# Linear attention and a gated FFN in one kernel: another order at the start and between the two parts, woven tiles in mid-sequence, and finish_b by pairs of groups

## The chip, the cores and the metric

The kernel runs on one core of one Trainium2 chip. The metric is the time of one execution in microseconds (us) on the device, less being better. Three runs of the kernel before gave a median of 2803.57 us (2799.61 to 2805.04). One further execution was profiled; it took 2802.45 us, of which the profiled span, from the first instruction to the last, is 2800.6 us.

The core has five engines with a queue each, which they work through in order: TensorE (PE in the profile: matmuls and transposes; its weight loads, PEld, overlap them), VectorE (DVE), ScalarE (ACT), GpSimd (POOL) and SyncE (SP), which here only issues DMAs. The other engines can issue DMAs too, from their own queues.

## The reference

The input x is 16 sequences of 1024 rows of 512 numbers. A linear attention with 16 heads of 32 comes first, then a gated FFN; after each, x is added and a layernorm is taken.

```python
qkv = x @ Wqkv.T + bqkv
q, k = rmsnorm(q, gq), rmsnorm(k, gk)             # over all 512
q, k = apply_rope(q), apply_rope(k)               # pairs (even, odd) by cos, sin
qf, kf = relu(q), relu(k)                         # 16 heads of 32
vk = einsum('bhlp,bhld->bhpd', [v, 1], kf)        # per sequence and head: 33 x 32
res = einsum('bhpd,bhld->bhlp', vk, qf)
attn = res[..., :-1] / (res[..., -1:] + 1e-6)
x = layernorm(x + rmsnorm(attn @ Wout.T + bout, gout))
# FFN; x_prev is x one row up, zero at a sequence's first row
xk = mu_k * x + (1 - mu_k) * x_prev
xr = mu_r * x + (1 - mu_r) * x_prev
out = layernorm(x + sigmoid(xr @ W_r.T) * (relu(xk @ W_k.T)**2 @ W_v.T))
```

## The kernel before

**Tiles and products.** The rows lie in N = 128 tiles of 128 rows; a sequence is 8 tiles, a group of the FFN NT = 4 tiles. Weights and activations are each split into a high and a low part in fp32r, and every product is three matmuls (high by high, high by low, low by high), usually 128x512, so 12 for a tile and a 512x512 weight. A cast on ACT makes the high part, a subtraction on DVE or POOL the low one. A scheduler puts the instructions of each engine in an order by its own simulated times; the program's order is its starting point. Eight semaphores serve the DMAs.

**Part one, `slot(i)` for each tile i (L563).** `proj` (L370) makes q and k of the tile: the bias has been copied into the PSUM bank by ACT before (`seeded`, L132, called the seed here), so the twelve matmuls add to it. `rope` (L417) squares q and k on ACT for the norm, multiplies them on DVE by two tables each (L425 into a tile called t2, L426 into ro), adds, and stores q to DRAM. The tables are the norm's weight times cos and sin. `tables(i)` (L394) computes them on POOL for the first eight tiles (L409, L412) and stores them in DRAM (tab_d, L413); from tile 8 on they are loaded (L404). `add_kx` (L449, matmuls pskx at L462) adds k^T x of tile i - 1 to a sum over the sequence, from the split k (kh on ACT, L438, kl on DVE, L439) and the split x (xnh, xnl). The four PSUM banks of that sum leave four banks, taken in turn, for everything else in part one.

**The end of a sequence.** v is never made per tile: `finish_a` (L472) copies the sum kx out of PSUM and splits it, `finish_s` (L480) makes the sum of k, `finish_b` (L494) multiplies by v's weights (pskv, L505 and L513), adds v's bias times the sum of k, applies the mask of heads and splits, in four column groups; `finish_c` (L531, psm at L538) multiplies one group each by the output weight and stores the result m in DRAM (m_d). In slots: finish_a and finish_s stand in the slot two after the sequence's last tile (9 + 8b for sequence b), finish_b in the next, finish_c in the four from 11 + 8b on.

**Woven tiles.** The attention's second step for a tile reads q and m back: `part_q` (L186, ends with L197 on DVE) divides by the denominator, `part_qt` (L201) transposes q (psqt, L138) and splits it (qth on ACT, L208, qtl on DVE, L209), `part_s` seeds the bank with the output bias, `part_m` multiplies by m (psy, L153), and `part_y` (L242) norms (the square on ACT is named junky, L247), adds x and takes the layernorm in place. For the first NPRE = 7 tiles this is begun inside part one: tile j's loads in slot FIRST + STEP j (40, 48, ...), part_q one slot later; for j < 4 the whole step follows there.

**The bridge.** After the last slot: w_k is loaded from DRAM, tiles 4 to 6 are completed, `turn` (L627) transposes x of group 0 (pst, L138) and `mix_t` (L633, ACT L637, DVE L638, split L648 and L649) makes the mixed x for k; the last sequence's ends stand between these and part_fk of group 0. Then w_r is loaded, group 0 is turned a second time for r, and tiles 7 and 8 are begun ahead with sequence 0's and 1's m.

**Part two.** For each group s, part_fk (psk), part_fr (psr) and part_fv (psv), all at L153, are woven with the attention's second step of the tiles two groups ahead (part_y's steps at L235 to L252) and with `part_t` (turn and both mixes) of the next group.

**The start.** In before, ACT's queue issues the loads of b_qk, of half of the weights, then of g_qk, cos, sin, b_out, g_out, mu and bv; the weights of q and then of k are split in four row blocks each (high part on ACT, low on POOL); then come tables(0) and seed(0).

Of the kernel before, what the change touches and what calls it, by code (L numbers as in the profile page):

```python
# [21 lines left out]
NPRE = 7  # L22
FIRST, STEP = 40, 8
XA = 7
XB = 4
# [8 lines left out]
def kernel(  # L34
# [221 lines left out]
    with ExitStack() as a_ctx:  # L256
# [49 lines left out]


# [5 lines left out]
        split_x(0)  # L313
        b_qk = ca.tile([P, 2 * DIM], F32, name="b_qk")
        nc.scalar.dma_start(out=b_qk, in_=bqkv[0 : 2 * DIM].partition_broadcast(P))
        for j in range(2):
            cols = slice(j * DIM, (j + 1) * DIM)
            for c in range(NC_):
                n = NC_ * j + c
                split_w(  # L320
                    w_qk["h"][:, c, cols],
                    w_qk["l"][:, c, cols],
                    wqkv[:, c, cols],
                    (V, G)[c % 2],
                    (nc.sync, nc.scalar)[c % 2],
                    *(("x", XA), ("q", 3))[n >= XA],
                )
        load_xt(1)
        load_xn(0)
        g_qk = wp.tile([P, 2 * DIM], F32, tag="m", bufs=NC_, name="g_qk")  # L330
        nc.scalar.dma_start(out=g_qk, in_=gqk.partition_broadcast(P))
        cos = ca.tile([P, 8, HH], F32, name="cos")
        nc.scalar.dma_start(out=cos, in_=cos_t)
        sin = ca.tile([P, 8, HH], F32, name="sin")
        nc.scalar.dma_start(out=sin, in_=sin_t)

        sn = ca.tile([P, 8, 2, HH], F32, name="sn")
        G.tensor_copy(sn[:, :, 0, :], sin)
        G.tensor_scalar(sn[:, :, 1, :], sin, -1.0, None, ALU.mult)
        nc.scalar.dma_start(out=b_out, in_=bout.partition_broadcast(P))  # L340
        nc.scalar.dma_start(out=g_out, in_=gout.partition_broadcast(P))
        mu, omm = {}, {}
        for n, m in (("k", mu_k), ("r", mu_r)):
            mu[n] = const.tile([P, NC_], F32, name=f"mu_{n}")
            nc.scalar.dma_start(out=mu[n], in_=m)
            omm[n] = const.tile([P, NC_], F32, name=f"omm_{n}")
            V.tensor_scalar(omm[n], mu[n], -1.0, 1.0, ALU.mult, ALU.add)

        bv = te.tile([P, NC_], F32, name="bv")
        with nc.allow_non_contiguous_dma(reason="512 numbers"):  # L350
            nc.scalar.dma_start(
                out=bv, in_=bqkv[2 * DIM : 3 * DIM].rearrange("(g p) -> p g", p=P)
            )
# [26 lines left out]
        first = {}  # L380

        def seed(i):
            for j in range(2):
                first[i, j] = seeded(f"ps{'qk'[j]}{i}", b_qk[:, j * DIM : (j + 1) * DIM])

        def rows(tl):
            return tl.rearrange("p (h i) -> p h i", i=HH)

        def halves(tl):
            return tl.rearrange("p (h two i) -> p h two i", two=2, i=HH)  # L390

        tab, tab_d = {}, {}

        def tables(i):  # L394

            t = i % 8
            if i < 8:
                tab_d[t] = dram.tile([P, 2, 2, DIM], F32, name=f"tab_d{t}")
            for j in range(2):
                for n in range(2):  # L400
                    tb = wa.tile([P, DIM], F32, tag=f"tab{j}{n}", name=f"tab{j}{n}{i}")
                    tab[i, j, n] = tb
                    if i >= 8:
                        nc.sync.dma_start(out=tb, in_=tab_d[t][:, j, n, :])  # L404
                        continue
                    g = g_qk[:, j * DIM : (j + 1) * DIM]
                    if n == 0:
                        c = cos[:, t, :].unsqueeze(1).to_broadcast([P, 2 * HEADS, HH])
                        G.tensor_mul(rows(tb), rows(g), c)  # L409
                    else:  # L410
                        c = sn[:, t, :, :].unsqueeze(1).to_broadcast([P, HEADS, 2, HH])
                        G.tensor_mul(halves(tb), halves(g), c)  # L412
                    nc.sync.dma_start(out=tab_d[t][:, j, n, :], in_=tb)  # L413

        acc, ros = {}, {}

        def rope(i, ps):  # L417
# [3 lines left out]
            for j in range(2):  # L421
                S.activation(junk(f"{i}{j}"), ps[j], AF.Square, accum_out=ss[:, j : j + 1])
                r = wa.tile([P, DIM], F32, tag=f"ro{j}", bufs=1 + j, name=f"ro{j}{i}")
                t2 = wa.tile([P, DIM], F32, tag="t2", name=f"t2{j}{i}")
                V.tensor_mul(t2, ps[j], tab.pop((i, j, 1)))  # L425
                V.tensor_mul(r, ps[j], tab.pop((i, j, 0)))  # L426
                V.tensor_add(halves(r), halves(r), halves(t2)[:, :, ::-1, :])
                ro.append(r)
                if j == 0:
                    q_d[i] = dram.tile([P, DIM], F32, name=f"q_d{i}")  # L430
                    nc.sync.dma_start(out=q_d[i], in_=r)
# [62 lines left out]
        def finish_b(b):  # L494
# [4 lines left out]
            for g in range(NC_):  # L499
# [4 lines left out]
                for c in range(NC_):  # L504
# [16 lines left out]
                kv = te.tile([P, P], F32, tag="kv", bufs=1, name=f"kv{b}{g}")  # L521
                V.scalar_tensor_tensor(
                    kv, ks[:, cols], bv[:, g : g + 1], ps[:, 0:P], ALU.mult, ALU.add
                )
                V.tensor_add(kv, kv, ps[:, P : 2 * P])
                V.tensor_mul(kv, kv, mask)
                S.copy(th[:, g, :], kv)
                V.tensor_sub(tl[:, g, :], kv, f32(th[:, g, :]))
# [30 lines left out]

        tables(0)  # L560
        seed(0)

        def slot(i):  # L563
            if i + 2 < N:
                load = load_xt(i + 2)
            b, t = divmod(i - 2, 8)
            if i - 2 >= 0 and t == 7:
                finish_a(b)
            if i < N:
                qk = [proj(i, 0), proj(i, 1)]  # L570
            if i + 1 < N:
                split_x(i + 1)
            if i < N:
                split_xn(i)
            if i + 1 < N:
                load_xn(i + 1)
            if i - 2 >= 0 and t == 7:
                finish_s(b)
            if i - 3 >= 0 and (i - 3) % 8 == 7:
                finish_b((i - 3) // 8)  # L580
            if i - 11 >= 0 and (i - 11) % 8 < NC_ and i < N:
                finish_c((i - 11) // 8, (i - 11) % 8)
            if 0 <= i - 1 < N:
                add_kx(i - 1)
            if i < N:
                state[i] = rope(i, qk)
            if i + 1 < N:
                tables(i + 1)
                seed(i + 1)
            if 1 <= i and late and i < N:  # L590
                late_weight()
            j, late_by = divmod(i - FIRST, STEP)
            if 0 <= j < NPRE:
                if late_by == 0:
                    with tc.issue_after(load.ins):
                        if j == 0:
                            load_ks(0)
                            for c in range(NC_):
                                load_m(0, c)
                        load_q(j)  # L600
                        load_x(j)
                    if j < NT:
                        part_s(j)
                if late_by == 1:
                    part_q(j)
                    if j < NT:
                        part_qt(j)
                        part_y(j, part_m(j))
# [55 lines left out]
        def part_fk(s, o):  # L664
# [10 lines left out]
            kh = wm.tile([P, HT], F32R, tag="kah", bufs=5, name=f"kah{s}{o}")  # L675
            kl = wm.tile([P, HT], F32R, tag="kal", bufs=5, name=f"kal{s}{o}")
# [4 lines left out]

        load_w("k", cb)
        for j in range(NT, NPRE):
            part_s(j)
        for c in range(NC_):
            turn(0, c)
            mix_t(0, c, "k")
        slot(N)
        for j in range(NT, NPRE):
            part_qt(j)  # L690
            part_y(j, part_m(j))
        slot(N + 1)
        part_fk(0, 0)
        part_fk(0, 1)
        slot(N + 2)
        part_fk(0, 2)
        part_fk(0, 3)
        tk_ctx.close()
        tx_ctx.close()
        wb = ctx.enter_context(tc.tile_pool(name="workb", reuse_waits="tile", bufs=1))  # L700
        wr = ctx.enter_context(tc.tile_pool(name="workr", reuse_waits="tile", bufs=1))
        own["ks"] = wr
        load_w("r", wr)
# [3 lines left out]
        )  # L707
        for g in range(NC_):
            finish_c(NB - 1, g)
        for c in range(NC_):  # L710
            turn(0, c)
            mix_t(0, c, "r")
        early = range(NPRE, 2 * NT + 1)
        load_ks(1)
        for j in early:
            load_q(j)
        load_q(2 * NT + 1)
        ps_m = {}
        for j in early:
            if j < 2 * NT:  # L720
                part_s(j)
            part_q(j)
            part_qt(j)
            if j < 2 * NT:
                ps_m[j] = part_m(j)

    wc = ctx.enter_context(tc.tile_pool(name="workc", reuse_waits="tile", bufs=1, side="right"))
    own["x"] = own["m"] = wc
    w_f["v"] = wc.tile([P, NC_, 2, DIM], F32R, name="w_v")

    def part_fr(s, t):
# [7 lines left out]
        gate[s, t] = wr.tile([P, DIM], F32, tag="gate", bufs=4, name=f"gate{s}{t}")  # L739
# [31 lines left out]
    for j in early:  # L771
        load_x(j)
    for c in range(NC_):
        load_m(1, c)
    for j in ps_m:
        part_y(j, ps_m[j])
    load_w("v", wc)
    for s in range(NH):
# [100 lines left out]
```

## Time and profile before

| | us |
|---|---|
| median of three runs | 2803.57 |
| profiled execution / its span | 2802.45 / 2800.6 |
| PE busy | 2728.1 (97%) |
| DVE / ACT / POOL busy | 2201.8 / 1893.1 / 735.8 |
| mean granted clock of PE | 0.994 |

A row of groups or of the timeline names the engine, the line, the operation and its output and inputs by the program's names. Of a wait, the engine, the tile and the instruction waited for are named. The granted clock is the share of full speed that the throttle gave PE in a window: 12 matmuls of 128x512 take 2.77 us at full clock and about twice that at half. The chain is the work that ended last, followed back from the end.

### The profile page before, as it was taken

How to read it: one execution, taken by the hardware profiler on the slowest of the kernel's cores; microseconds unless marked ns; L12 is line 12 of the kernel's file. 1: busy time of each engine (PE TensorE's matmuls, PEld its weight loads, DVE VectorE, ACT ScalarE, POOL GpSimd, SP SyncE). 2: the span in 40 equal slices, each digit the busy share in tenths (PEclk: the TensorE clock that was granted, in tenths of full speed). 3: DMA queues.
4: the chain of work that ended last, by engine and by line, in shares of the span. 5: the costliest groups of instructions: out<-in, count | busy, mean ns of one | idle time of the engine just before them, and what ended most of it. 6: DMA issues, size and time to landing. Idle time of an engine off the chain costs nothing.

```text
span 2800.6 us, 40329 instructions
## 1 busy us (share of the span) xinstructions
PE 2728.1 (97%) x12536; PEld 2236.0 (80%) x12536; DVE 2201.8 (79%) x4966; ACT 1893.1 (68%) x3839; POOL 735.8 (26%) x808
## 2 busy tenths in 40 slices
PE   7999999999999999988999999999999999999998
PEld 5788877777888888866788888888888888888887
DVE  7988877777888788866778787878787878788774
ACT  5566655555555566655777777777777777777775
POOL 6422221221222222222322222222222222222221
PEclk9999999999999999999999999999999999999999
DMA  7787776666777777755323222232323132313210
GB/s 245 234 294 254 236 256 204 213 209 202 231 237 238 237 230 237 231 176 176 104 70 106 95 77 92 92 110 65 106 91 113 57 113 84 110 65 106 76 57 30
DMA packets 230854, 431.17 MB, mean 154 GB/s; under 512 B 24544, under 2 KB 24800, under 8 KB 230640
## 3 DMA queue, kind: packets, MB, share of 16 engines
q1 hardware_dynamic: 228384, 425.85, 46.9%
q10 hardware_dynamic: 2256, 2.76, 0.3%
q8 instruction: 99, 1.62, 0.2%
q14 instruction: 115, 0.94, 0.1%
HBM read 313.14 MB, written 115.38 MB: 153 GB/s over the span
## 4 chain that ended last, share of the span: by engine, by line
PE 76%; DVE 1%; DMA 1%; ACT 1%; issue 0%; POOL 0%; SPq 0%; POOLq 0%; ACTq 0%; DVEq 0%
PE psk L153 13%; PE psv L153 12%; PE psy L153 12%; PE psr L153 12%; PE pskx L462 7%; PE psq L370 7%; PE psk L370 7%; PE pst L138 2%; PE psqt L138 2%; PE psm L538 1%; PE pskv L505 1%; DMA m_d<-m 0%; DMA w_r<-w_dr 0%; PE pskv L513 0%; DMA mb<-m_d 0%
## 5 line engine op out<-in xcount | busy, mean ns | idle before, releaser
L153 PE MATMUL psk<-mkh,w_k 128*128 128x512 f32 x1024 | 337.3, 396 | 0.0
L153 PE MATMUL psr<-w_r,mrh 128*128 128x512 f32 x1024 | 325.9, 400 | 2.6 <-issue 2.6
L153 PE MATMUL psv<-w_v,kah 128*128 128x512 f32 x1024 | 326.4, 400 | 1.5 <-DVE qtl L209 1.5
L153 PE MATMUL psy<-mb,qth 128*128 128x512 f32 x1024 | 319.8, 393 | 2.3 <-ACT qth L208 1.4
L117 POOL TENSOR_TENSOR rstd_all<-ss,mhalf 128x2 f32<-128x2 f32 x128 | 119.1, 931 | 685.6 <-DVE ss L432 666.7
L245 DVE TENSOR_TENSOR y<-psy,g_out 128x512 f32<-128x512 f32 x128 | 88.5, 691 | 187.3 <-PE psy L153 186.6
L370 PE MATMUL psq<-wqk_h,xh 128*128 128x512 f32 x512 | 204.1, 399 | 26.2 <-ACT psq L132 26.2
L153 PEld LDWEIGHTS psy<-mb,qth 128*128 128x128 f32 x1024 | 192.6, 189 | 46.3 <-ACT qth L208 2.2
L153 PEld LDWEIGHTS psk<-mkh,w_k 128*128 128x128 f32 x1024 | 192.3, 188 | 39.4
L153 PEld LDWEIGHTS psr<-w_r,mrh 128*128 128x128 f32 x1024 | 189.5, 190 | 40.1 <-issue 2.8
L153 PEld LDWEIGHTS psv<-w_v,kah 128*128 128x128 f32 x1024 | 187.9, 188 | 41.9 <-DVE qtl L209 1.9
L649 POOL TENSOR_TENSOR mkl<-mixk,mkh 128x512 fp32r<-128x512 f32 x128 | 175.6, 1372 | 150.2 <-ACT mkh L648 150.2
L462 PE MATMUL pskx<-kl,xnh 128*128 128x512 f32 x512 | 203.1, 397 | 5.6 <-DVE kl L439 5.5
L370 PE MATMUL psq<-wqk_l,xh 128*128 128x512 f32 x512 | 203.8, 398 | 0.0
L370 PE MATMUL psq<-wqk_h,xl 128*128 128x512 f32 x512 | 203.7, 398 | 0.0
L462 PE MATMUL pskx<-kh,xnl 128*128 128x512 f32 x512 | 202.2, 395 | 0.0
L153 PE MATMUL psv<-w_v,kal 128*128 128x512 f32 x512 | 202.1, 395 | 0.0
L370 PE MATMUL psk<-wqk_h,xh 128*128 128x512 f32 x512 | 200.4, 391 | 1.8 <-ACT psk L132 1.8
L153 PE MATMUL psy<-mb,qtl 128*128 128x512 f32 x512 | 201.6, 394 | 0.0
L153 PE MATMUL psr<-w_r,mrl 128*128 128x512 f32 x512 | 201.5, 394 | 0.0
L370 PE MATMUL psk<-wqk_h,xl 128*128 128x512 f32 x512 | 200.2, 391 | 0.0
L370 PE MATMUL psk<-wqk_l,xh 128*128 128x512 f32 x512 | 199.8, 390 | 0.0
(148 smaller groups left out, 7248.9 us busy)
## 6 DMA issues: line engine op xcount, KB each, us to landing
tab<-tab_d SPq DMA_DIRECT2D x480, 256.0 KB
xt<-in_xt_dram SPq DMA_DIRECT2D x128, 256.0 KB
xn<-in_x_dram SPq DMA_DIRECT2D x128, 256.0 KB
q_d<-ro SPq DMA_DIRECT2D x128, 256.0 KB
m_d<-m SPq DMA_DIRECT2D x64, 512.0 KB
mb<-m_d SPq DMA_DIRECT2D x64, 512.0 KB
q<-q_d SPq DMA_DIRECT2D x128, 256.0 KB
x<-in_x_dram SPq DMA_DIRECT2D x128, 256.0 KB
```

The source lines that it names most:

```text
L117: G.tensor_tensor(dst, src, mhalf[:, 0 : src.shape[1]], ALU.pow)
L138: T.matmul(ps[:, n * P : (n + 1) * P], lhsT=b, rhs=ident, is_transpose=True, start=(n == 0), stop=(n == NC_ - 1), skip_group_check=True,)
L153: T.matmul(ps, lhsT=a[u][:, rows], rhs=b[w][:, cols], start=(afresh and c == 0 and k == 0), stop=(c == n - 1 and k == 2), skip_group_check ...
L245: V.tensor_mul(y, ps, g_out)
L370: T.matmul(ps, lhsT=a[i][:, c, :], rhs=w_qk[b][:, c, cols], start=False, stop=(c == NC_ - 1 and n == 2), skip_group_check=True,)
L462: T.matmul(ps_kx[b][c], lhsT=a[:, cols], rhs=r, start=(t == 0 and n == 0), stop=(t == 7 and n == 2),)
L505: T.matmul(ps, lhsT=w_a["h"][:, c, cols], rhs=kx[:, c, g, :, :].rearrange("p two n -> p (two n)"), start=(g % 2 == 0 and c == 0), stop=Fal ...
L538: T.matmul(ps, lhsT=a[:, g, :], rhs=w_o[r][:, g, :], start=(n == 0), stop=(n == 2))
L649: (V if n == "r" and s != 1 else G).tensor_sub(ml, m, f32(mh))
```

## The change

Six things are changed together.

1. **Woven tiles.** NPRE is 8, FIRST is 44, and NDONE = 5 tiles are completed in part one (in slots 44, 52, 60, 68, 76 and the ones after); of tiles 5, 6 and 7 only part_q is. The ring of x has 8 outer and 3 inner buffers rather than 7 and 4.
2. **The start.** The load of b_qk is issued ahead of the first split. The seed of tile 0 and tables(0), with the loads of g_qk, cos and sin, stand between the weights of q and those of k. b_out, g_out, mu and bv are loaded by SP in slot 2 (`constants`). The late weights begin at slot 5 rather than 1. The table with sin is made ahead of the one with cos.
3. **t2 in place.** rope's first product is written over its table rather than into a tile of its own.
4. **finish_b by pairs.** After the multiplication of each group (128 wide), the addition, the mask, the cast and the subtraction are done once for two groups (256 wide).
5. **The bridge.** Both w_k and w_r are loaded first. The order is then tile 5, add_kx(127), finish_a, tile 6, finish_s, finish_b, part_t of group 0 (one transposition for both mixes), tile 7, finish_c, then the loads for tiles 8 and 9, and part_fk of group 0. Tile 8 is begun just ahead of the loop of part two.
6. Pools follow: workr is gone, its tiles lie in workb and workc.

```diff
-NPRE = 7
-FIRST, STEP = 40, 8
-XA = 7
-XB = 4
+NPRE = 8
+FIRST, STEP = 44, 8
+NDONE = 5
+XA = 8
+XB = 3
...
         load_xt(0)
-        split_x(0)
         b_qk = ca.tile([P, 2 * DIM], F32, name="b_qk")
         nc.scalar.dma_start(out=b_qk, in_=bqkv[0 : 2 * DIM].partition_broadcast(P))
+        split_x(0)
...
         for j in range(2):
             cols = slice(j * DIM, (j + 1) * DIM)
             for c in range(NC_):
...
+            if j == 0:
+                seed(0)
+                nc.scalar.dma_start(out=g_qk, in_=gqk.partition_broadcast(P))
+                nc.sync.dma_start(out=cos, in_=cos_t)
+                nc.sync.dma_start(out=sin, in_=sin_t)
+                G.tensor_copy(sn[:, :, 0, :], sin)
+                G.tensor_scalar(sn[:, :, 1, :], sin, -1.0, None, ALU.mult)
+                tables(0)
...
-                for n in range(2):
+                for n in (1, 0):
                     tb = wa.tile([P, DIM], F32, tag=f"tab{j}{n}", name=f"tab{j}{n}{i}")
...
-                t2 = wa.tile([P, DIM], F32, tag="t2", name=f"t2{j}{i}")
-                V.tensor_mul(t2, ps[j], tab.pop((i, j, 1)))
+                t2 = tab.pop((i, j, 1))
+                V.tensor_mul(t2, ps[j], t2)
                 V.tensor_mul(r, ps[j], tab.pop((i, j, 0)))
                 V.tensor_add(halves(r), halves(r), halves(t2)[:, :, ::-1, :])
...
-                V.tensor_add(kv, kv, ps[:, P : 2 * P])
-                V.tensor_mul(kv, kv, mask)
-                S.copy(th[:, g, :], kv)
-                V.tensor_sub(tl[:, g, :], kv, f32(th[:, g, :]))
+                if g % 2 == 1:
+                    two = slice(g - 1, g + 1)
+                    low = both.rearrange("p (g two n) -> p g two n", g=2, two=2)[:, :, 1, :]
+                    V.tensor_add(kv, kv, low)
+                    V.tensor_mul(kv, kv, mask.unsqueeze(1).to_broadcast([P, 2, P]))
+                    S.copy(th[:, two, :], kv)
+                    V.tensor_sub(tl[:, two, :], kv, f32(th[:, two, :]))
...
-            if 1 <= i and late and i < N:
+            if i == 2:
+                constants()
+            if i >= 5 and late:
                 late_weight()
...
         load_w("k", cb)
-        for j in range(NT, NPRE):
-            part_s(j)
-        for c in range(NC_):
-            turn(0, c)
-            mix_t(0, c, "k")
-        slot(N)
-        for j in range(NT, NPRE):
-            part_qt(j)
-            part_y(j, part_m(j))
-        slot(N + 1)
-        part_fk(0, 0)
-        part_fk(0, 1)
-        slot(N + 2)
-        part_fk(0, 2)
-        part_fk(0, 3)
+        load_w("r", cb)
+        y5 = rest(NDONE)
+        add_kx(N - 1)
+        part_y(NDONE, y5)
         tk_ctx.close()
-        tx_ctx.close()
...
-        load_w("r", wr)
+        finish_a(NB - 1)
         pa_ctx.close()
...
+        part_y(NDONE + 1, rest(NDONE + 1))
+        finish_s(NB - 1)
+        finish_b(NB - 1)
+        tx_ctx.close()
+        wb = ctx.enter_context(tc.tile_pool(name="workb", reuse_waits="tile", bufs=1))
+        for c in range(NC_):
+            part_t(0, c)
+        part_y(NDONE + 2, rest(NDONE + 2))
         for g in range(NC_):
             finish_c(NB - 1, g)
-        for c in range(NC_):
-            turn(0, c)
-            mix_t(0, c, "r")
-        early = range(NPRE, 2 * NT + 1)
...
-    for j in early:
-        load_x(j)
+    first = 2 * NT
+    load_q(first)
+    load_q(first + 1)
+    load_ks(1)
     for c in range(NC_):
         load_m(1, c)
-    for j in ps_m:
-        part_y(j, ps_m[j])
+    load_x(first)
+    for o in range(NC_):
+        part_fk(0, o)
     load_w("v", wc)
+    part_q(first)
+    part_qt(first)
```

`rest(j)` is part_s, part_qt and part_m of tile j.

## The prediction

> **What bounds the kernel now.** I read the page's first part, then the windows, then what TensorE (PE) waited for, then the places themselves.
>
> ```profile
> PE 2728.1 (97%) x12536; PEld 2236.0 (80%) x12536; DVE 2201.8 (79%) x4966; ACT 1893.1 (68%) x3839; POOL 735.8 (26%) x808
> ```
>
> PE is the bound with 97%. The change removes hardly any matmuls, so it can only win the idle 72.5 us, what a half clock costs beside it, and a few transposes. The windows (time, PE, PEld, DVE, ACT and POOL busy, granted clock, DMA share) say where these lie.
>
> ```profile
> 0.00:100.00 100.00, 77.11 (x298) 58.94 (x298) 80.69 (x99) 50.45 (x102) 71.00 (x57) 0.98 0.69 235
> 100.00:200.00 100.00, 97.42 (x441) 78.74 (x442) 85.34 (x152) 65.01 (x138) 22.36 (x20) 1.00 0.87 289
> 200.00:400.00 200.00, 200.00 (x911) 165.11 (x912) 161.04 (x289) 120.68 (x256) 48.13 (x42) 1.00 0.77 246
> 400.00:500.00 100.00, 91.74 (x406) 74.08 (x405) 78.39 (x149) 56.84 (x122) 19.58 (x19) 0.98 0.67 212
> 500.00:600.00 100.00, 93.65 (x430) 76.78 (x429) 72.73 (x147) 55.12 (x119) 20.79 (x21) 0.98 0.61 195
> 600.00:700.00 100.00, 96.11 (x432) 78.50 (x431) 76.86 (x150) 57.61 (x126) 21.27 (x21) 0.98 0.69 220
> 700.00:1200.00 500.00, 500.00 (x2285) 413.04 (x2284) 407.99 (x731) 299.19 (x643) 113.06 (x102) 1.00 0.73 233
> 1200.00:1300.00 100.00, 85.07 (x385) 66.97 (x384) 65.58 (x137) 57.31 (x114) 25.64 (x25) 0.93 0.52 174
> 1300.00:1400.00 100.00, 93.87 (x424) 76.18 (x425) 74.76 (x203) 71.99 (x141) 36.27 (x41) 0.97 0.38 126
> 1400.00:2700.00 1300.00, 1300.00 (x6113) 1071.46 (x6112) 1043.18 (x2777) 995.05 (x1966) 337.49 (x435) 1.00 0.28 90
> ```
>
> Three places lose time: the start (25.5 us idle to 200), the four woven tiles (8.26 + 6.35 + 3.89 = 18.5 idle in 400 to 700) and the bridge between the parts (14.93 + 6.13 = 21.1 in 1200 to 1400). A clock of 0.93 over 100 us is 7 us of lost work, 0.98 about 2. The end of the span loses another 6.8 and is not touched. Elsewhere PE is full: the sequence ends after 700, with no woven tile, cost nothing.
>
> What PE waited for, in us, times, longest:
>
> ```profile
> PE psq L370 <- ACT psq L132: 26.2, 8, 12.7
> PE pskx L462 <- ACT kh L438: 7.8, 6, 1.9
> PE pskx L462 <- DVE kl L439: 5.5, 8, 1.4
> PE psqt L138 <- DVE q L197: 5.3, 2, 3.5
> PE pst L138 <- DVE mixk L638: 3.8, 2, 2.2
> PE psr L153 <- issue: 2.6, 1, 2.6
> ```
>
> **The change part by part.**
>
> *Woven tiles (FIRST 44, five done).* Tile j's last step (psqt, psy) falls in before on the slot after a sequence's end, where ACT and DVE also have finish_a, finish_s and finish_b. The timeline of the first (start, duration) shows the wait that closes each:
>
> ```profile
> 432.35 0.60 ACT L422 ACTIVATE junk<-psq 128x512 bf16<-128x512 f32 x1
> 432.93 0.59 ACT L132 COPY psq<-b_qk 128x512 f32<-128x512 f32 x1
> 433.57 0.50 PE L370 MATMUL psq<-wqk_h,xh 128*128 128x512 f32 x1 [1.99 <-ACT psq L132]
> ```
>
> The four places, added up by hand: 3.5 + 0.62 + 1.99, then 1.91 + 0.62 + 1.99, 1.13 + 0.62 + 1.99, 1.27 + 0.62 + 2.00. In the new order pskx waits no longer (1.1 to 1.9), since kh no longer stands behind finish_a and finish_s; nor does pskv (0.62), which isn't there. The seed's wait remains: psy takes the last of four banks, ACT's square of psy (0.60 + 0.19) frees it, and the seed copy (0.59) follows. In the new order PE follows psy with psm (three matmuls, 0.7 us), while ACT does psm's cast (0.6, once psm is done), then the square (0.79) and the seed (0.59): with 0.15 for hand-overs the next psq starts 2.85 us after psy, 2.15 of it idle; five times is 10.8. The granted clock fell to half for 3.41 us at 412.48, 514.88 and 678.72, that is at three of four weaves; a half window loses 1.7. With two or three in five, 3.4 to 5: about 14.5 in place of 18.5 + 3 x 2 = 24.5. **Gain 10**; bounds 4 (the pskx waits stay, five stalls of 4) to 15 (no half clock).
>
> The Trainium skill, "TensorE: Matmul & The Clock Gate", Part 1, lets the clock fall after an idle window of some 3.4 us. The rows differ: after 1.99 us idle (513.2 to 515.23) and 2.00 (676.4 to 678.38) it was half at once, after another 1.99 (597.45) not. By the page no new weave would slow the clock, and the sum would be 4 us lower.
>
> *finish_b by two groups.* A sequence loses six DVE instructions and two ACT casts (128 wide, 0.28 to 0.29 each); the rest double in width. PE lost nothing at the ends between 700 and 1200, so 15 of 16 are covered by PE's full queue: 0. If that cover were gone, it would still be a gain, under 1.7 us a sequence. The last one counts in the bridge.
>
> *The bridge.* Before, PE turned x twice for k and r (8 groups of 4 transposes), waited on mixk and on q (L197) three to four times, and the chain ran through three DMAs in a row:
>
> ```profile
> 1284.72 9.03 DMA w_r<-w_dr
> 1293.82 9.12 DMA m_d<-m
> 1303.96 6.95 DMA mb<-m_d
> ```
>
> Now w_r is asked for right behind w_k, before the last sequence ends, so its 9.03 is over some 25 us before its first use. The store and reload of m (9.12 + 6.95) is hidden behind what now stands between: part_fk(0) with 48 matmuls (4 x 2.77 us) and the psy of tile 7 (2.77). The m_d store lands, by the walk, 35 us after psk of tile 127, and mb is needed at 40. Four turns go: 4 x 0.5 = 2.0. Removed: 21.1 idle, 10 by the clock (0.93 and 0.97), 2.0. What is late next: kx(127) waits for nothing at first, since tile 5's mixing work stands ahead (0 to 1); the transposes qt of tiles 6 and 7 wait for DVE (1.3 and 1.3); the small products of finish_c wait for the mixing work of part_t on ACT and DVE (2); psy of tile 8, which is no longer made ahead, waits for its qth (1.5 to 2). Sum 7.5, with one or two half windows 10.5 to 11. **Gain 33 - 11 = 22.** Bounds: 28 (only 5 lost) and 6, if each of the five hand-overs between DVE, ACT and PE costs as much as the longest of before (3.5 + 1.7 each).
>
> *The start.* Before, the first real matmul is at 17.96, behind the seed at 17.3, which stands in ACT's queue behind the constants' DMAs; the clock is half until 23.36, and tiles 0 and 1 are done at 31.5. Now b_qk (landed at 5.67) comes ahead of k's weights and the seed is at about 7; first matmul 8.5. But POOL, in order, gets the first tables between q's and k's low halves, and the first of these waits for g_qk (11.5 to 12, estimated from an issue 2 to 3 us earlier than the row's 7.64 to 14.19). With 1.75 us for each table and 1.26 for each low half, k's last comes at 22.4, and tiles 0 and 1 end at 23.3 to 25. Then the seed of tile 2 follows four ACT steps: 27.5 to 29. Gain here 3, with bounds 2.5 and 8.
>
> Against it stands t2, now written over its table, in tiles 1 to 8. The store of that table must have landed first:
>
> ```profile
> L409 POOL TENSOR_TENSOR tab<-g_qk,cos x16: 1264/1738/1845, 17.0 to 94.2; 128x512 f32<-128x512 f32 x16
> L413 SPq DMA_DIRECT2D tab_d<-tab x32: 319/383/457, 19.8 to 97.0; - x32
>   DMA tab_d<-tab: 0.9, 2
> ```
>
> The two k tables are made one after the other once DVE has released the old ones (2 x 1.75), the store is issued (0.4) and lands 2.0 to 3.5 us later, and then only DVE multiplies. With the four DVE steps between, the round is 10 to 11 us; before, a slot took 10.1 us between 31.5 and 102.5, with 8.3 of PE's work. What is queued behind the waiting multiplication on DVE: ro, the add, ss, kl, and through kl PE's pskx; on ACT the next seed. Six slots by 0 to 1 us: 3 lost, bounds -2 (the table is made first, so its round may be shorter) and +11. **Start: 0**, between -6 (gain) and +8.
>
> The Trainium skill, "DMA: Bandwidth & Descriptors", Anatomy of one DMA, gives a fixed 2.0 us and 436 GB/s, which makes 2.6 for such a store; the trace's stores took 2.0 to 4.6 with other transfers beside them. By the page's value the start would gain 3.
>
> *In-place t2 from tile 8 on.* The table comes back by a load. Its buffer is freed by the add (1.0 us after ro's multiplication, 3.2 at most) rather than by t2's multiplication. A load issued at 917.6 landed at 921.6, and its reader began at 925.0: 3.4 us to spare. So 0 for 119 slots, hidden by PE's 8.3 us a slot; no gain is possible where PE is full. If the cover were gone, each slot would pay up to 1.0.
>
> *Constants at slot 2, late weights from slot 5:* DMAs on SP (issue 0.4 each, seven of them) go past tab's stores once: at most 2.8 us in one slot of the start, counted in its upper bound. The weights are still taken in early, as nothing before holds them. XA 8 and XB 3 put all eight first weight pieces in x's ring; k's pieces landed one after the other up to 11.74 before, in the same order as now: 0.
>
> **Sum** against the profiled execution: 2802.45 (span 2800.6 + 1.85), 1.1 below the median of the runs, 2803.57. 2802.45 - 10 - 22 + 0 = 2770.5; I take 2770.
>
> **The rivals.**
>
> *The bridge stays a ping-pong* (20%): PE is quick and has one tile's work at a time; DVE at 66% and ACT at 57% in 1200 to 1300 speak for queues in order rather than for work as its limit. Then the bridge gains 6 and the start loses 2: 2788.
>
> *The start gains fully* (13%): stores land in 2 us and the tables made first are early enough; -6 and a weave of 12: 2762.
>
> *Slower* (13%): the in-place tables. If t2's later release pushes SP's load, and so t2's next multiplication, past its time in the steady part, DVE is the bound for 119 slots. Each 0.1 us costs 12 us; it decides from 32 / 119 = 0.27 us a slot. DVE's 82% in 700 to 1200 speaks for it, the 3.4 us to spare against it. At 0.35 us: 2812.
>
> *Nothing is won* (6%): the psy square and the seed cost each of the five weaves the old 6 us (+6), and the bridge only 6: 2802.
>
> **How the numbers follow.** My case (48%) has 2757 to 2785 by its bounds taken partly together. Down to 2752 the range holds the start's gain with a good bridge; up to 2799 the ping-pong with the start's loss of 8 and weaves that gain 6. That leaves out the last two rivals and little else. Within 0.2% (5.6 us, about what a measurement of this kernel can tell) is the fourth and a bit of the first. Faster 48 + 13 + 19 = 80%, same 6 + 1 = 7%, slower 13%.
>
> **What would show it.** Right: psq's first wait about 8 us in place of 17.96; five waits of psq on the seed of 2 us between 400 and 800, no pskx wait there; no w_r, m_d or mb in the chain; PE busy over 91 in 1200 to 1300. Wrong: DVE's t waiting on a tab DMA beyond slot 8, PE under 99% in 800 to 1200, tile 8's first multiplication after 108 (102.7 before), or psqt, pst and psm waits above 12 us in the bridge.

## The result

The kernel after took 2819.66 us (median of four runs, 2811.05 to 2822.91) against 2802.98 for the kernel before: 1.0056 times, with a 95% interval of 1.0037 to 1.0075. That is 17 us slower, where 33 us of gain had been forecast. The profiled execution has a span of 2817.6 us.

The page's first part and the windows of the profile after (from and to, length, then PE, PEld, DVE, ACT and POOL busy, granted clock, DMA share, GB/s):

```profile
PE 2742.2 (97%) x12520; PEld 2235.6 (79%) x12520; DVE 2187.8 (78%) x4870; ACT 1886.8 (67%) x3807; POOL 729.4 (26%) x808
```

```profile
0.00:100.00 100.00, 79.65 (x287) 57.92 (x288) 74.84 (x95) 49.12 (x100) 66.47 (x55) 0.91 0.67 225
100.00:200.00 100.00, 92.65 (x406) 74.07 (x404) 74.85 (x127) 57.97 (x120) 22.60 (x21) 0.98 0.78 248
200.00:400.00 200.00, 196.05 (x893) 160.35 (x894) 160.55 (x280) 118.78 (x253) 43.77 (x40) 1.00 0.78 246
...
700.00:1200.00 500.00, 490.09 (x2198) 399.24 (x2197) 387.22 (x681) 288.91 (x612) 109.36 (x102) 0.99 0.71 224
1200.00:1300.00 100.00, 97.32 (x463) 79.77 (x462) 76.98 (x143) 60.83 (x127) 25.07 (x25) 1.00 0.69 220
1300.00:1400.00 100.00, 90.85 (x418) 72.78 (x417) 76.94 (x183) 72.09 (x142) 37.44 (x39) 0.98 0.37 120
```

The loss has moved. The stretch from 200 to 400, where PE had been busy 200.00 us of 200, has a hole of 4 us, and that from 700 to 1200 one of 10 (with one woven tile more in it). The clock of the first 100 us (0.91 here, 0.98 before) can't be compared by this column: before's trace has no clock record ahead of 23.36, where its matmuls ran one per 0.43 us, and one per 0.23 from then on. PE is busy 14 us more than before although it has 16 matmuls fewer. Half clocks count as busy, and from 100 us to tile 127 there are nine steps at half clock rather than three. Only the bridge, which now lies in 1250 to 1340, is better: the two last lines leave 11.8 us idle there, before 21.1.

A stage is best read by when a tile's first psq matmul starts, in the profiled executions:

| first psq matmul of tile | before | after | difference |
|---|---|---|---|
| 0 | 17.96 | 7.55 | -10.4 |
| 2 | 31.48 | 31.39 | -0.1 |
| 9 | 102.53 | 107.73 | +5.2 |
| 20 | 211.28 | 221.49 | +10.2 |
| 41 | 399.04 | 413.69 | +14.7 |
| 86 (all woven tiles done) | 851.33 | 884.33 | +33.0 |
| 127 | 1225.78 | 1263.39 | +37.6 |
| end of the span | 2800.6 | 2817.6 | +17.0 |

Of the 33 at tile 86, some 3.3 us are work that moved: tile 4's 12 psy matmuls and 4 transposes, done in the bridge before. So part one lost 34 us and the bridge won 17 (20.6 less that 3.3).

What DVE and PE waited for in the profile after (us, times, longest):

```profile
DVE tab L432 <- DMA tab<-tab_d: 56.1, 36, 4.7
DVE tab L432 <- DMA tab_d<-tab: 1.6, 3, 0.9
```

```profile
PE psq L412 <- ACT psq L133: 22.2, 16, 6.3
PE pskx L469 <- DVE kl L446: 8.1, 9, 3.0
PE pskx L469 <- ACT kh L445: 7.5, 8, 1.8
PE pskv L512 <- DVE kx L484: 6.9, 5, 1.5
```

The first line is new: before, the multiplication into t2 stood behind a table's load for no time worth a row. L432 is the in-place t2; the second line is its wait for the table's own store at the start. The last of PE's lines is a wait at the sequence ends that before did not have either (there pskv waited 2.5 us in all, on ACT's junky). The in-place wait is the rival that the prediction gave 13%. A sequence end just behind a woven tile shows it (start, duration):

```profile
492.95 0.68 DVE L432 TENSOR_TENSOR tab<-psq,tab 128x512 f32<-128x512 f32 x1
493.55 0.67 DVE L433 TENSOR_TENSOR ro<-psq,tab 128x512 f32<-128x512 f32 x1
494.15 0.67 DVE L432 TENSOR_TENSOR tab<-psk,tab 128x512 f32<-128x512 f32 x1
494.74 0.67 DVE L433 TENSOR_TENSOR ro<-psk,tab 128x512 f32<-128x512 f32 x1
495.34 0.67 DVE L434 TENSOR_TENSOR ro<-ro,tab 128x512 f32<-128x512 f32 x1
...
496.42 0.42 SPq L332 DMA_DIRECT2D tab<-tab_d  x1
...
501.27 0.69 DVE L432 TENSOR_TENSOR tab<-psq,tab 128x512 f32<-128x512 f32 x1 [3.19 <-DMA tab<-tab_d]
...
510.75 0.36 PE L512 MATMUL pskv<-kx,wa_h 128*128 128x256 f32 x1 [1.50 <-DVE kx L484]
```

q's table is read at 492.95, but k's two multiplications go between it and the add (495.34), which now is the last reader of the buffer. The next load goes out at 496.42 rather than behind t2's own multiplication, which ended at 493.6, and takes 4.8 us to land; the next tile's psq, begun at 496.76, is finished before the table is there. DVE idles 3.19 us with the add, kl and the sequence end's kx (L484) behind it, and nine microseconds later PE waits for kx.

### The profile page after: what moved, and what is told of

It reads as the page before. It is cut to its first block, busy times and chain, and to the rows that moved or that the text cites. A ratio compares the mean times of both kernels' runs of the same rounds, so it can differ in the third digit from the quotient of the medians.

```text
span 2817.6 us, 40017 instructions
## 1 busy us (share of the span) xinstructions
PE 2742.2 (97%) x12520; PEld 2235.6 (79%) x12520; DVE 2187.8 (78%) x4870; ACT 1886.8 (67%) x3807; POOL 729.4 (26%) x808
## 4 chain that ended last, share of the span: by engine, by line
PE 52%; DVE 0%; ACT 0%; issue 0%; POOL 0%; POOLq 0%; ACTq 0%
PE psv L154 12%; PE psk L154 12%; PE psr L154 12%; PE psy L154 12%; PE pst L139 2%; PE psqt L139 2%; ACT x L241 0%; DVE x L744 0%; ACT junkf L236 0%; DVE nma L240 0%; POOL rsa L118 0%; DVE x L253 0%; DVE gate L742 0%; DVE den L193 0%; DVE pr L191 0%
## 5 line engine op out<-in xcount | busy, mean ns | idle before, releaser
L118 POOL TENSOR_TENSOR rstd_all<-ss,mhalf 128x2 f32<-128x2 f32 x128 | 113.3, 885 | 688.8 <-DVE ss L439 674.0
L154 PE MATMUL psk<-mkl,w_k 128*128 128x512 f32 x512 | 200.4, 391 | 0.4 <-POOL mkl L657 0.4
```

Source lines behind the costliest of these rows:

```text
L118: G.tensor_tensor(dst, src, mhalf[:, 0 : src.shape[1]], ALU.pow)
L154: T.matmul(ps, lhsT=a[u][:, rows], rhs=b[w][:, cols], start=(afresh and c == 0 and k == 0), stop=(c == n - 1 and k == 2), skip_group_check ...
```

## The experiments

Times are medians; the kernel before was run beside each group (2801.8, 2801.9, 2803.5, 2802.7, 2802.2).

**t2 in its own tile again** (all else as after; the tile comes from the ring of y, which has two buffers).

```diff
-                t2 = tab.pop((i, j, 1))
-                V.tensor_mul(t2, ps[j], t2)
+                t2 = tp.tile([P, DIM], F32, tag="y", bufs=2, name=f"t2{j}{i}")
+                V.tensor_mul(t2, ps[j], tab.pop((i, j, 1)))
```

> The kernel after, with t2 again in a tile of its own (in the ring of y, two buffers), all else as after. Theory A (in place, the table's buffer is released late, its next load lands late and DVE's multiplication waits for it: 56.1 us in 36 times in the profile of after): the loss of the start from tile 8 on, of 200 to 300 and at the sequence ends behind the weaves goes, some 20 to 25 us of the 35 that part one lost: 2793 to 2800, and DVE's wait for a tab load falls below 10 us. Theory B (the woven tiles in mid-sequence take DVE and ACT too much time just ahead of a sequence's end): within 4 us of after, about 2818, the pskv waits of 1.25 to 1.5 us at the sequence ends stay.

2777.53 (0.9913 of before, 0.9899 to 0.9928): **42 us** less than after. That is 15 us below theory A's range. DVE's wait for loaded tables at this line is down from 56.1 to 5.1 us (another 2.3 at ro's), and the pskv wait is gone from PE's list. Of the 31 us that after loses to this kernel between tiles 9 and 127, 16 are idle time of PE (33.1 against 17.2); half clocks, nine against three, make about 10 (an estimate: 3.41 us each, at half speed). Whether the ring's second buffer has a share in the 42 us was not separated.

```profile
DVE t L432 <- DMA tab<-tab_d: 5.1, 7, 1.6
```

The start shows the other half of the same wait. The first t2 of all ran at 19.65 in this kernel. In after it stood until the table's store, issued at 22.41, had landed at 29.07, 6.7 us later; the bank, the seed on ACT and tile 2 stood behind it. Profile after, then this kernel:

```profile
22.41 1.53 SPq L341 DMA_DIRECT2D tab_d<-tab  x2
...
29.16 0.69 DVE L432 TENSOR_TENSOR tab<-psq,tab 128x512 f32<-128x512 f32 x1 [0.31 <-DMA tab_d<-tab]
...
31.39 0.80 PE L412 MATMUL psq<-wqk_h,xh 128*128 128x512 f32 x1 [6.31 <-ACT psq L133]
```

```profile
24.38 0.50 PE L412 MATMUL psq<-wqk_h,xh 128*128 128x512 f32 x1 [0.87 <-ACT xh L279]
```

**Only t2 in place, on the kernel before** (the third part of the change alone).

> The kernel before, with only t2 written in place over its table (tables still in the order cos, sin). Theory A: 10 to 20 us slower than before, 2813 to 2823, and DVE waits for tab loads as in after. Theory B: as before, within 3 us of 2803.

2824.66 (1.0078, 1.0061 to 1.0095), 23 us slower: slightly above theory A's range, far from B. DVE's waits there, on loads and on stores of tables:

```profile
DVE tab L425 <- DMA tab<-tab_d: 37.7, 30, 4.1
DVE tab L425 <- DMA tab_d<-tab: 2.8, 6, 0.6
```

**Only FIRST 44, on the kernel before** (one number changed).

> The kernel before, with only FIRST 44 (four tiles done in mid-sequence). Theory A: the gain that was predicted for four weaves, 8 to 10 us: 2793 to 2796. Theory B: the weaves cost more than before, 2806 to 2816, with pskv waiting on DVE at the sequence end behind each weave.

2788.88 (0.9953, 0.9938 to 0.9967): 13 us faster and 4 below theory A's range; theory B falls. Each of the four weaves keeps one stall of psq on the seed, where 2.15 us were predicted; the pskx and pskv waits at the weaves are gone, and no weave has a half clock. The first of the four:

```profile
465.02 0.50 PE L370 MATMUL psq<-wqk_h,xh 128*128 128x512 f32 x1 [1.89 <-ACT psq L132]
```

**After with the whole start of before** (t2 in place), and **after with only cos first again**:

```diff
-                for n in (1, 0):
+                for n in range(2):
```

> The kernel after, with the whole start of before (order of seed, tables and constants, cos table first, late weights from slot 1); t2 stays in place. If the start itself loses the 5 us by tile 9 and the 9 by tile 11: 2808 to 2812. If these come from the in-place table (theory A): within 4 us of after, 2814 to 2820.

> The kernel after (t2 in place, new start), with only the order of the two tables put back: cos ahead of sin. The old start with t2 in place took 2796.5, 23 less than after, and it changed this order, the seed's and tables' place and the late weights' slot together. Theory A1 (the order decides: the sin load, which must wait for the add, stands ahead of the cos load on SP's queue and holds it and what follows up): 2796 to 2803. Theory A2 (the rest of the start decides, such as tables(0) ahead of k's weights): within 4 us of 2819.

2796.47 and 2809.86, each outside both of its ranges. With t2 in place the order of the tables is worth 10 us, less than A1 gave, and the rest of the start 13 more. How the order acts is not shown: with cos first DVE's wait on loaded tables is no shorter (58.0 us against 56.1).

**After with the late weights from slot 1** isolates the third part of the start:

```diff
-            if i >= 5 and late:
+            if i >= 1 and late:
```

> The kernel after (t2 in place, sin table first), with the late weights allowed from slot 1 as before. With t2 in place the old start took 2796.5, the new one with cos first 2809.9. If the late weights' place is what the in-place table cannot stand (their stages' loads stand on SP ahead of the tables' stores in slots 5 to 10): 2804 to 2812. If it is the place of tables and seed: 2815 to 2822.

2799.51: 20 us less than after, below the range that was given. Half of it is there by tile 26 (265.05 against 274.91), the rest comes later, when both kernels have all weights. DVE's wait on loaded tables falls:

```profile
DVE tab L432 <- DMA tab<-tab_d: 38.4, 27, 3.4
```

**The same questions with t2 apart**: the old start, the old place of the weaves, and late weights from slot 1 (the last on the kernel with the early ksb, below).

> The kernel with t2 in its own tile (2777.5) and the whole start of before. With t2 apart, tile 9 began at 96.8 rather than 102.5, and tile 41 at 393.7 rather than 399.0, so the new start is worth about 5.5 us if nothing else plays in: 2781 to 2785. If that lead is the t2 ring's (two buffers in place of one): 2775 to 2779.

> The kernel with t2 in its own tile, and the woven tiles back at slot 40 (five done). By the theory that the place of the weaves matters as predicted (6.1 us of idle each at a sequence's end rather than 2 to 3, and half clocks): 2785 to 2795, with pskx waits on kh of 1 to 2 us and pskv waits of 0.62 back. If the place does not matter without the in-place table: 2775 to 2780.

> The kernel with t2 in its own tile and the early ksb load (2769.8), with the late weights from slot 1 rather than 5. If their slot costs only together with the late release: 2767 to 2772. If it costs by itself: below 2762.

2779.68, 2782.13 and 2777.67, against 2777.53 for the first two and 2769.83 for the third. The first two lie between their two ranges, the third above both. So with t2 apart the new start is worth 2 us in the end (it leads by 7 at tile 9: 96.82 against 103.82, and gives most of that back), the place of the weaves 5, and late weights from slot 1 *cost* 8: the 20 us above are not the late weights' own. The 10 and the 20 us also don't add up with the 23 of the whole start: these parts act on each other.

**finish_b by groups again**, with t2 apart; and **by pairs on the kernel before**:

> The kernel with t2 in its own tile, and finish_b group by group as before. Predicted value of the pairs: 0, so 2775 to 2780. If fewer, wider DVE instructions shorten the sequence ends (at most 1.7 us at each of 16): up to 2800. If the wider steps come later and cost: 2765 to 2774.

> The kernel before, with finish_b by pairs only. The theory of the ksb load has nothing to act on here, as the old bridge loads ksb later and waits for other things: within 3 us of 2802. If pairs are slower at the sequence ends by themselves: 2806 to 2812.

2770.53, 7 us below the run with pairs; on before, 2808.54 (1.0017, 1.0008 to 1.0026), 5 above its 2803.49. Yet tile 127 starts within 0.8 us in the first pair (1220.41 and 1221.16) and 0.3 in the second (1226.06 and 1225.78): the sequence ends cost nothing, and the loss is in the bridge. So 2808.54 lies in the second range of its expectation, but not for the reason given there. On before, the bridge with pairs has a longer wait for mb, the reload of m, in its one profiled execution (2812.85): 5.37 us, before's being 0.94.

```profile
1315.40 1.22 PE L153 MATMUL psy<-mb,qth 128*128 128x512 f32 x2 [5.37 <-DMA mb<-m_d]
```

With t2 apart the timelines of the bridge, with pairs and then without, differ so:

```profile
1268.99 0.56 SPq L172 DMA_DIRECT2D ksb<-ks_d  x1
...
1275.30 2.38 DVE L191 SCALAR_TENSOR_TENSOR pr<-q,ksb 128x512 f32<-128x512 f32 x2 [6.22 <-DMA ksb<-ks_d]
...
1281.83 0.44 PE L139 MATMUL pst<-ident,x 128*128 128x128 f32 x1 [4.56 <-DVE mixr L646]
```

```profile
1266.06 0.56 SPq L172 DMA_DIRECT2D ksb<-ks_d  x1
...
1270.16 2.37 DVE L191 SCALAR_TENSOR_TENSOR pr<-q,ksb 128x512 f32<-128x512 f32 x2 [2.19 <-DMA ksb<-ks_d]
```

Sequence 1's ksb load stands on SP behind the last sequence's four stores of m, and DVE's part_q of tile 8 waits for it, with the mixed x for PE behind. **The load at the head of the bridge**, into the buffer of sequence 0's:

```diff
-        ksb[b] = ring("ks", b, 1, 1, [P, DIM], F32, f"ksb{b}")
+        ksb[b] = ring("ks", max(b - 1, 0), 1, 1, [P, DIM], F32, f"ksb{b}")
...
+        load_ks(1)
         load_w("k", cb)
         load_w("r", cb)
```

> The kernel with t2 in its own tile (2777.5, pairs in finish_b), with sequence 1's load of ksb issued at the beginning of the bridge, into the buffer of sequence 0's, rather than behind the last sequence's four stores of m. Theory: the pairs cost 7 us only because the last store of m goes out 2.9 us later on SP, ksb behind it lands 3.8 us later, and DVE's pr of tile 8 (6.2 us idle) holds up the mixed x, on which PE waits 4.56: 2768 to 2773. Rival: the pairs themselves are slower at each end: 2775 to 2778.

> The same with finish_b group by group (2770.5 without the early load). DVE's wait on ksb there is 2.2 us: by the theory 2767 to 2770, and equal to the run with pairs within 3 us; by the rival 2767 to 2770 and 6 us or more below it.

2769.83 (0.9877, 0.9860 to 0.9893) with pairs, the fastest kernel of the study with the 2770.53 above; 2774.96 with groups. The first is as the theory has it: 7.7 us come back, and nothing waits for ksb there. The second is above all of its ranges: without pairs the early load *costs* 4.4. That profile has two other waits in the bridge, psv 3.15 and psy 2.80 us, each with a half clock (from 1291.64 and 1301.88). So a few us of the bridge hang on the order that comes out, and were not settled further.

**Is it the release, or the order of instructions?** On before with t2 in place, a second buffer for q's sin table alone; then for both (a buffer of the x ring is given up: NPRE 6), with its control.

```diff
-                    tb = wa.tile([P, DIM], F32, tag=f"tab{j}{n}", name=f"tab{j}{n}{i}")
+                    tb = wa.tile([P, DIM], F32, tag=f"tab{j}{n}", bufs=1 + n, name=f"tab{j}{n}{i}")
```

(`1 + (j == 0 and n == 1)` in the first.)

> The kernel before with t2 in place (2824.7 against 2802 without), and two buffers for q's sin table alone. Of DVE's waits ahead of t2's multiplication in the steady part, 27 of 40 us stand at q's (10.5 of 12 before) and 13 at k's (1.5 before). If the late release is the cause: most of q's share goes, 2806 to 2815, and DVE's wait on tab loads falls from 37.7 to below 20. If the order of instructions is the cause and not the release: 2820 to 2827.

> The kernel before with t2 in place, two buffers for both sin tables, NPRE 6 and rings XA 6, XB 5. If the late release is the whole cause: within 4 us of its control, and from tile 20's first matmul to tile 127's as before, 1014.5 us (2 us more at most; 1029.9 with t2 in place, 1022.8 with q's second buffer). If the order of instructions does the rest: 8 to 16 us above the control, and 1022 us or more.

> The kernel before with NPRE 6 and rings XA 6, XB 5, t2 in its own tile. Only the bridge has another tile to fetch: 2800 to 2812, and 1014 to 1016 us between the first matmuls of tiles 20 and 127.

| | time, us | DVE on loaded tables | tile 20 to tile 127, us |
|---|---|---|---|
| before | 2802 | under 1 | 1014.5 |
| t2 in place | 2824.66 | 37.7 | 1029.9 |
| q's table twice | 2818.39 | 15.4 | 1022.8 |
| both twice (NPRE 6) | 2804.59 | none | 1020.3 |
| control (NPRE 6) | 2792.51 | none | 1015.3 |

With q's buffer alone 2818.39 lies between the two ranges, and the wait on loaded tables fell as the release theory has it:

```profile
DVE tab L425 <- DMA tab<-tab_d: 15.4, 9, 4.4
```

With both, 2804.59 is 12 us above the control, where the release as the whole cause allowed 4; the other theory (8 to 16, and 1022 us or more between the tiles) has that number, but not the 1020.3. The control itself came out 7.5 us below its range, by the bridge. With both buffers doubled the wait is gone altogether, and 9.6 of the 15.4 us that the steady part had lost come back. The last 5, and 4 in the bridge (1570.1 us from tile 127 to the end, the control 1566.0), stay. The late release is thus shown for about 10 of the 15 in the steady part and 10 to 11 of the 23 in all (2824.66 less 2802, against 2804.59 less 2792.51). The rest is spread in pieces of about 1 us per 100 us between 200 and 900, with no table wait beside them; one step more at half clock (five against the control's four) makes about 1.7 of it. Whether the other order of instructions makes them was not tried by itself and stays open.

## Where the prediction was right and wrong

*t2 in place from tile 8 on, priced at 0 with "up to 1.0" a slot if the cover were gone: wrong, and the step that decided.* From tile 9 to tile 127 the kernel after took 1155.7 us and the one with t2 apart 1124.3: 31 us, 0.27 a slot, just the value from which the prediction's slower rival decides. (How much of such a loss is the late release was measured on before alone: 10 of 15 us.) The error is in the two numbers of that step. The release was put 1.0 us later, 3.2 at most, counted from ro's multiplication, and 1.0 was used; where k's two come between, it is 2.4 later than t2's own (which ends at 493.6, the add at 496.0). The 3.4 us to spare were read at one place in the middle of a sequence, where PE sets the pace, and by the trace's semaphores the two loads issued there at 916.96 and 917.55 landed at 922.27 and 922.91 rather than 921.6, 2.7 us ahead of their readers. At the place shown above the load went out 2.8 us after t2's multiplication and was 3.2 us late: there was nothing to spare. The prediction's first sign of being wrong, t waiting on a table's DMA beyond slot 8, is the 56.1 us.

*The start, 0 within -6 and +8: inside its bounds at +5.2 by tile 9, but for a wait not priced at that place.* The first matmul (8.5 predicted, 7.55) was right, and so was the end of tiles 0 and 1 (23.3 to 25 predicted, 25.1 in after, 23.5 with t2 apart). Tile 2, expected at 27.5 to 29, begins at 24.38 with t2 apart but at 31.39 in after: the very first t2 waits for a store too. Stores were taken at 2.0 to 3.5 us, from slots 0 to 8; this one, among the weights' loads, took 6.7, and the other three of tile 0's tables 5.4 to 5.9 (before's stores, all in all, 2.0 to 4.6). The 2.6 us that the prediction sets beside them comes from a fit that the Trainium skill, "DMA: Bandwidth & Descriptors", Anatomy of one DMA, gives for DMAs issued by GpSimd; these go out from SyncE. Nor did the tables with sin come first for tile 0: its two with cos were made at 11.38 and 12.61, the two with sin at 19.00 and 20.27.

*The late weights at slot 5, at nothing:* 20 us with t2 in place, -8 without. An interaction; its mechanism was not shown.

*Woven tiles, a gain of 10: the mechanism right, alone (13 on before), but only 5 with t2 apart and the rest of the change.* The stall of psq was 1.89 for 2.15. (The sum put 2 us on each half clock of before, where its own figure is 1.7.) Not foreseen: a wait of psy on qth of 0.68 at each weave once t2 is apart, and in after the sequence ends behind each weave (DVE 3.19 and 1.9 idle, pskv 1.25 to 1.5), where the in-place table bites. With t2 apart those waits are gone; the old place of the weaves with t2 in place was not run.

*finish_b by pairs, 0: right for the sequence ends* (0.3 and 0.8 us). Its 5 to 7 us arise in the bridge, where the prediction gave the last one no price.

*The bridge, a gain of 22: the mechanism right, the size 17.* w_r, m_d and mb are no longer waited for. What was late next was not on the list: ksb's load behind the stores of m, 4.9 us of DVE in after. With the early load 1548.2 us pass from tile 127 to the end, against 1574.8 before: 26.6 less, 23 without the work that moved.

*The sum.* -10 - 22 + 0 was forecast. Measured in after: part one +34, the bridge -17. Two bounds don't follow from their terms, and neither mattered: the start's best case is -10 (8 and 2), not -6, and five hand-overs of 5.2 us leave the bridge 7, not 6. Without t2 in place the change gives 24 us, and 34 with the early load.

## What to carry to other kernels

Writing a result over an input saves a tile and moves the release of that input to the result's last reader; where the input comes by a prefetch of one buffer, count from that reader through the queue and the landing to the next use, and count it at the crowded places, not at one quiet place of the steady part. A table that is also being stored can't be overwritten before its store has landed, and in the crowded start here that took 6.7 us, two to three times what had been counted. An edit whose own cost is nothing can still move a load behind stores on a queue that works in order: look for what the waiting instruction holds up.

## What the hardware showed

The granted clock goes by a grid of 3.41 us: in each profile all its changes lie on one such grid, which lies differently from run to run. The woven tiles in mid-sequence give 54 equal stalls in eleven profiles (1.88 to 1.89 us: after, the same with late weights from slot 1, cos first or the old start, FIRST 44 on before, and six kernels with t2 apart). Of the 30 that lay wholly inside one step of the grid, 29 were followed by a step at half clock; of the 24 that a step's border cut, 23 were not, and the other one was cut by 0.02 us. The line is a fine one: of the stalls that were cut, five had 1.81 to 1.87 us inside one step and no half clock. For the kernel with t2 apart:

| psq starts after its stall | half clock from |
|---|---|
| 461.92 | none (the border at 460.24 cuts the stall, 1.68 us are behind it) |
| 541.51 | 542.16 |
| 622.74 | 624.08 |
| 704.00 | none (border at 702.58) |
| 783.62 | 784.50 |

The Trainium skill, "TensorE: Matmul & The Clock Gate", Part 1, calls the window free-running, and the runs agree; its idle window of some 3.4 us as the condition is too long, since 1.89 us inside one window were enough. Whether such a stall costs 1.9 or some 3.6 us (an estimate: the stall and half of a step of 3.41) is a matter of where it falls. In after all five fell inside, and a half clock followed each; on before with FIRST 44 none of four.
